# A two-layer convolution block: order of loads and buffers at the seams between passes and in the 7x7 convolution's own steps

## The chip, the core and the metric

The kernel runs on one core of a Trainium2 chip. The core has a matrix engine (TensorE, "PE" in the profile, with its weight loads as "PEld"), a vector engine (VectorE, "DVE"), a scalar engine (ScalarE, "ACT"), GpSimd ("POOL") and SyncE ("SP"), each with its own instruction stream, worked off in the order in which it was written. They wait for one another through semaphores. Transfers between on-chip memory (SBUF) and device memory are started from a stream, here SP's or POOL's (few from ACT's), and are moved by 16 DMA engines. TensorE writes its results to PSUM, in banks of 512 floats per partition, from where another engine evicts them. The metric is the device time of one execution in microseconds (us); lower is better.

## The reference

The input x is 8 images of 96 x 96 points with 192 channels, float32. Two layers are added to it in turn, each of them behind a group norm with 32 groups of six channels.

```python
x = x + layer0(group_norm(x))
x = x + layer1(group_norm(x))

# layer0: 192 -> 384 channels
proj  = v @ W_in + b_in
local = depthwise 3x3 convolution of proj
mixed = 0.25 * (scan right + scan left + scan down + scan up of local) + local
        # scan: s = 0.6 * s + 0.4 * value, along a row or a column
out   = layer_norm(mixed) * ln_g + ln_b, then @ W_out + b_out      # 384 -> 192

# layer1: 192 channels
y = depthwise 7x7 convolution of v, + dw_bias
y = layer_norm(y) * ln_gamma + ln_beta
y = gelu(y @ w0 + b0) @ w1 + b1                                     # 192 -> 768 -> 192
out = y * gamma
```

## The kernel before, in words

The program is a row of passes that hand their data on through device memory[...]. Line numbers are those of the kernel before.

**Pass A** takes the first group norm's figures, normalises and projects to 384 channels, and writes the projection to `P_d`. Per block `k` of rows and per image `b`, `store_a` (L411) issues three whole stores (one per 128 channels, 1152 KB each) and, in the first and the last block, a store of the rows at the blocks' edge (L428), all from POOL.

**Pass B** does the 3x3 convolution as matmuls against banded weight matrices (`conv_b`, L600), 12 channels at a time. `load_b` (L576) reads a banded matrix and, in three pieces, a tile `pin` of `P_d`: the main rows, then one row at each edge, from SP, three blocks ahead. VectorE runs the scans down and up (L633, L642), further matmuls apply the sideways scans as a matrix (L621, L624), and `store_steps` (L644) writes `M_d` from POOL, at the end from SP and POOL.

**Pass C** runs over 192 units u: `load_c` (L984) reads a tile `mt` of `M_d` and a tile `xr` of x, three units ahead, from SP. TensorE transposes and projects (L1008, L1010), ScalarE takes the layer norm's squares (L1014), VectorE forms the new x, in a tile `x1c` of two buffers (L1027), and `store_c` writes it to `X1_d` from SP in pieces of 384 KB (L1063), one per unit. At the head of the pass, inside the pool `c_prep`, weights and norm factors are read and folded into `wc` and `cst` (L949 to L975).

**The own steps.** The 7x7 convolution is again done with banded matrices. The list `todo` has 32 steps: two halves of four images, 16 blocks of 12 channels in each. The first N1 = 19 steps (NI = 16 are one half) stand between pass C and the MLP; the others are mixed into the MLP. A step n has these parts:

- `load_raw(n, t)`, t = 0, 1, 2: rows of x from `X1_d`, half from SP, half from POOL, 384 KB each;
- `scale_steps(n)`: 24 operations that apply the second group norm (tile `xin`, two buffers by parity of n), on VectorE (L841) but for the first and the last of the own steps, where ScalarE does them (L839); and `spread` (L845), which copies the banded matrix to the other 64 partitions on VectorE;
- `load_band(n)` (L820): the banded matrix, 64 partitions x 2496 floats, from SP or POOL by parity. Its tile comes from one of two pools, by parity of n;
- `conv_d(n, c)`, c = 0 to 5: 24 matmuls each (L1168) into two banks, and two evictions on ScalarE (L1178) into `yo`. There are eight banks;
- `store_d(n)`: three stores of `yo` to `Y_d` from SP and three from POOL (L1194, L1198, L1199).

The loop over n that puts these in order begins at L1428. In turn n it stores step n-1, loads the band of n+1 and the rows of n+2, writes the scalings and the spread of n+1, and then the matmuls and evictions of n. In turns 16 and 18 it also writes `load_y` (L1206), which reads the convolved rows back from `Y_d` in 40 small pieces from SP, seven per `conv_d`. In turns 17 and 18, ahead of the matmuls, it writes the first steps of the MLP's layer norm, `norm_steps_e` (L1257): sums, mean, center on VectorE, square on ScalarE, squares on VectorE, powers on POOL, scale on VectorE. The first six or seven of these precede the matmuls of that turn.

Band 0 and the rows of step 0 are read inside pass C, at 20 units before its end, and the rows of step 1 in its last 14 units; the scalings of step 0 are there too.

**The MLP** (L1369, L1379, L1399) runs over tiles of the convolved rows, with the steps 19 to 31 of the convolution in its first half.

In all parts around the change, the order within an engine is the order in which the Python program writes its instructions (`manual_schedule`). Where a pool gives a tile the place of an earlier one, the new tile's first writer waits for the last users of the old one, tile by tile (`reuse_waits="tile"`); where tiles of different pools come to lie on the same bytes, the same holds.

Of the kernel before, what the change touches and what calls it, by code (L numbers as in the profile page):

```python
# [101 lines left out]
def conv_blocks_kernel(  # L102
# [31 lines left out]
    nc = tc.nc  # L134
# [103 lines left out]
    with ExitStack() as ph:  # L238
# [173 lines left out]
        def store_a(po, b, k):  # L412
            at, g = b % GB, b // GB
            for m in range(NC):
                nc.gpsimd.dma_start(
                    P_d[
                        g, m * 128 : (m + 1) * 128, k * WA : (k + 1) * WA, at
                    ].rearrange("p r j h -> p r (j h)"),
                    po[:, m].rearrange("p r j h -> p r (j h)"),
                )  # L420

            for edge, r, row, js in (
                (NK - 1, WA - 1, RB, (0, NJ - 1)),
                (0, 0, RB + 1, (1, NJ)),
            ):
                if k == edge:
                    to = slice(1 - js[0], NJ - js[0])
                    nc.gpsimd.dma_start(  # L428
                        P_d[g, :, row, at, to].rearrange("(m p) j h -> p m (j h)", p=128),
                        po[:, :, r, js[0] : js[1]].rearrange("p m j h -> p m (j h)"),  # L430
                    )

# [128 lines left out]
    by_tile = dict(reuse_waits="tile")  # L561
    with ExitStack() as ph:
# [103 lines left out]
        with tc.manual_schedule():  # L666
# [10 lines left out]
            for n in range(NI * (n_k + 1)):  # L677
                k, i = divmod(n, NI)
                z = None
                if k < n_k:  # L680
# [133 lines left out]
    def load_band(n):  # L814

        i = todo[n][1]
        pool = d_pools[0 if n >= N1 else n % 2]
        bands[n] = band = pool.tile([128, GC, ZW], F32, tag="band", name="band1")
        g = i % 2
        (nc.sync, nc.gpsimd)[g and n < N1].dma_start(  # L820
            band[g * 64 : (g + 1) * 64].rearrange("q c l -> q (c l)"),
            Z2_d[:, i * GC : (i + 1) * GC].rearrange("r c l -> r (c l)"),
        )

    def scale_steps(n):
# [4 lines left out]
        def scale(t, k, b):  # L830
# [7 lines left out]
            if n == 1 or n >= N1 - 1:  # L838
# [17 lines left out]
    gn_pool = ExitStack()  # L856
    gp = gn_pool.enter_context(tc.tile_pool(name="gn", bufs=1, side="right", **by_tile))
# [70 lines left out]
    with ExitStack() as ph:  # L928
# [20 lines left out]
        with tc.tile_pool(name="c_prep", bufs=1, **by_tile) as pp:  # L949
            wo = pp.tile([128, NC, D], F32, name="wo")  # L950
            nc.sync.dma_start(wo, W_out.rearrange("(m p) d -> p m d", p=128))
            gb = pp.tile([128, 2, NC], F32, name="gb")
            with nc.allow_non_contiguous_dma(reason="one value per partition"):
                nc.sync.dma_start(gb[:, 0], ln_g.rearrange("(m p) -> p m", p=128))
                nc.sync.dma_start(gb[:, 1], ln_b.rearrange("(m p) -> p m", p=128))
            bo = pp.tile([128, D], F32, name="bo")
            nc.sync.dma_start(bo, b_out.partition_broadcast(128))
            mean_w = pp.tile([128, 128], F32, name="mean_w")
            nc.vector.memset(mean_w, 1.0 / C)
            lnb = pp.tile([128, NC, 128], F32, name="lnb")  # L960
            ps = ps_s.tile([128, 512], F32, tag="gn_ps", name="ps_w")
            for m in range(NC):
                nc.vector.tensor_scalar(wc[:, m, :D], wo[:, m], gb[:, 0, m : m + 1], None, ALU.mult)
                nc.vector.tensor_copy(lnb[:, m], gb[:, 1, m : m + 1].to_broadcast([128, 128]))
            for m in range(NC):
                nc.tensor.matmul(
                    ps[:, :D], mean_w, wc[:, m, :D], start=(m == 0), stop=(m == NC - 1)
                )
            for m in range(NC):
                nc.tensor.matmul(  # L970
                    ps[:, D : 2 * D], lnb[:, m], wo[:, m], start=(m == 0), stop=(m == NC - 1)
                )
            for m in range(NC):
                nc.vector.tensor_tensor(wc[:, m, :D], wc[:, m, :D], ps[:, :D], ALU.subtract)
            nc.vector.tensor_tensor(cst, bo, ps[:, D : 2 * D], ALU.add)  # L975
# [96 lines left out]
        with tc.manual_schedule():  # L1072
            weights = load_weights()
            for u in range(n_u + 1):
# [7 lines left out]
                if u == n_u - 20:  # L1082
                    load_band(0)
                    for t in range(NT):
                        load_raw(0, t)
# [337 lines left out]
    with tc.manual_schedule():  # L1423
        with tc.tile_pool(name="d_own", bufs=1, side="right", **by_tile) as own:
            d_pools[1] = own
            load_band(1)
            norms, chain = norm_c(1, bank), []
            for n in range(N1):  # L1428
                if n:
                    store_d(n - 1)  # L1430
                    if n + 1 < N1:
                        load_band(n + 1)
# [4 lines left out]
                if n + 1 < N1:  # L1437
                    if n + 2 < N1:
                        for t in range(NT):
                            load_raw(n + 2, t)  # L1440
                    for step in scale_steps(n + 1):
                        step()
                if n >= NI + 1:
                    chain = norm_steps_e(n - NI - 1)
                    for _ in range(7 if n == NI + 1 else 6):
                        chain.pop(0)()
                parts = load_y((n - NI) // 2) if n in (NI, NI + 2) else []
                for c in range(GS):
# [131 lines left out]
```

## Time and profile before

| | |
|---|---|
| time, median of three runs | 5589.31 us (5582.28 to 5594.85) |
| profiled execution | 5586.89 us, its span 5585.1 us |
| PE busy | 5299.5 us (95%), 42206 matmuls |
| DVE, ACT, POOL busy | 3594.6 (64%), 2594.4 (46%), 2326.4 us (42%) |
| DMA | 1015.29 MB, mean 182 GB/s |
| pass A, B, C | to 757, 766 to 1797, 1813 to 2627 us |
| own steps, MLP | 2627 to 3021, 3021 to 5585 us |

The profile is of one execution. Times count from the start of its span. In its lists of waits a line gives the engine, the tile it was about to write and the line of the program, then what ended the wait (engine or DMA and its tile), the total in us, how often, and the longest. In a table of windows the columns are the stretch, its length, the busy time of each engine with the number of instructions, the clock that TensorE was granted as a share of full speed, the mean busy share of the DMA engines and the rate they moved. A share of DMA can come out a little over 1. In the slices, each digit is the busy share of one fortieth of the span in tenths (9 is 90% or more).

### The profile page before, as it was taken

Reading aid. Unit: us, or ns where it says so; the run is one execution under the profiler, and the core shown is the slowest. Engines: PE = TensorE matmul, PEld = TensorE weight load, DVE = VectorE, ACT = ScalarE, POOL = GpSimd, SP = SyncE. Lnnn points to the kernel's source line nnn. Section 1 sums busy time; section 2 is a strip of 40 time slices with the busy share of each in tenths; the row PEclk is TensorE's granted clock in tenths of the full one; section 3 lists DMA queues with packets and bytes.
Section 4 is the critical chain, followed back from the end, with each engine's and each line's share of the span. In section 5 each row is a group of like instructions: output and inputs, shape, how many; then the busy total and the mean of one; then the engine's idle time right before and its main releaser. Section 6 shows DMA issues by size and latency. Waiting matters only on the chain. (4 is left out here: it accounts for less than half of the span.)

```text
span 5585.1 us, 108130 instructions
## 1 busy us (share of the span) xinstructions
PE 5299.5 (95%) x42206; PEld 3348.2 (60%) x42206; DVE 3594.6 (64%) x6714; ACT 2594.4 (46%) x5786; POOL 2326.4 (42%) x2037
## 2 busy tenths in 40 slices
PE   6999989999998999998775999999999999999999
PEld 4666643333333999997342655666566676667667
DVE  6656449999998455555543655555566676766764
ACT  2444447777776566565333444444433233333332
POOL 1111128888887555554321232232233333333332
PEclk9999989999999999999887999999999999999999
DMA  7999869999997899999995554565433332233331
GB/s 217 285 289 268 239 197 245 243 247 243 243 247 207 262 293 288 281 288 270 276 271 130 120 121 110 126 137 140 110 88 92 81 81 77 79 88 90 81 79 40
DMA packets 800700, 1015.29 MB, mean 182 GB/s; under 512 B 331345, under 2 KB 683282, under 8 KB 798141
## 3 DMA queue, kind: packets, MB, share of 16 engines
q1 hardware_dynamic: 712005, 672.30, 47.4%
q0 software_dynamic: 82224, 333.85, 18.4%
q8 instruction: 333, 5.46, 0.4%
q10 hardware_dynamic: 5960, 2.22, 0.2%
q14 instruction: 178, 1.46, 0.1%
HBM read 603.70 MB, written 419.95 MB: 183 GB/s over the span
## 5 line engine op out<-in xcount | busy, mean ns | idle before, releaser
L1399 PEld LDWEIGHTS hp<-w1g,g 128*128 128x128 f32 x6912 | 1118.6, 190 | 141.2 <-issue 73.2
L1399 PE MATMUL hp<-w1g,g 128*128 128x192 f32 x6912 | 1175.6, 329 | 0.0
L1388 ACT ACTIVATE g<-hp,b0g 128x512 f32<-128x512 f32 x864 | 518.3, 690 | 1144.4 <-PE hp L1379 1144.4
L1418 POOL DMA_DIRECT2D out_dram<-xo x288 | 210.5, 731 | 1641.6 <-DVE xo L1410 1546.5
L1369 PE MATMUL hp<-yT,w0w 128*128 128x512 f32 x1728 | 780.8, 598 | 16.0 <-DVE yT L1354 12.1
L1410 DVE TENSOR_TENSOR xo<-hp,r 128x384 f32<-128x384 f32 x288 | 227.6, 790 | 815.2 <-PE hp L1399 806.4
L1010 PE MATMUL po<-wc,mt 128*128 128x193 f32 x3456 | 684.5, 334 | 1.9 <-DVE x1c L1027 1.8
L600 PE MATMUL pl<-pin,band 34*32 34x380 f32 (+1 forms) x13824 | 628.9, 489 | 18.8 <-DMA pin<-P_d 18.8
L674 POOL TENSOR_TENSOR mo<-mo,z 128x768 f32<-128x768 f32 x286 | 598.7, 2093 | 2.7 <-ACT mo L625 0.2
L1168 PE MATMUL hp<-xin,band 63*64 63x372 f32 (+1 forms) x4608 | 441.8, 521 | 154.7 <-DVE band L845 53.4
L1010 PEld LDWEIGHTS po<-wc,mt 128*128 128x128 f32 x3456 | 554.4, 191 | 33.0 <-ACT mean L1012 30.6
L1369 PEld LDWEIGHTS hp<-yT,w0w 128*128 128x128 f32 x1728 | 322.1, 191 | 377.4 <-issue 339.0
L633 DVE TENSOR_TENSOR_SCAN z<-decay,loc 128x768 f32<-128x768 f32 x288 | 505.8, 1756 | 40.8 <-ACT loc L609 11.8
L642 DVE TENSOR_TENSOR_SCAN z<-decay,z 128x768 f32<-128x768 f32 x288 | 498.4, 1731 | 0.1
L600 PEld LDWEIGHTS pl<-pin,band 34*32 34x32 f32 x13824 | 232.8, 107 | 396.8 <-issue 394.8
L1333 POOL TENSOR_TENSOR rs<-tot,neg_half 32x32 f32<-32x32 f32 x72 | 394.6, 5481 | 112.5 <-DVE tot L1331 112.4
L621 PE MATMUL pa<-loc,mix 128*32 128x384 f32 x3456 | 431.8, 493 | 0.0
L624 PE MATMUL pa<-last,down 96*32 96x384 f32 x1152 | 426.7, 493 | 0.9 <-ACT mo L625 0.9
L1168 PEld LDWEIGHTS hp<-xin,band 63*64 63x64 f32 x4608 | 209.7, 145 | 357.5 <-issue 240.4
L1379 PE MATMUL hp<-yT,w0w 64*128 64x512 f32 x1728 | 419.7, 611 | 0.0
L1178 ACT ACTIVATE yo<-hp,dwb 128x384 f32<-128x384 f32 x384 | 200.3, 576 | 437.3 <-PE hp L1168 359.1
L609 ACT COPY loc<-pl 128x384 f32<-128x384 f32 x576 | 248.1, 483 | 311.6 <-PE pl L600 311.6
(158 smaller groups left out, 7524.2 us busy)
## 6 DMA issues: line engine op xcount, KB each, us to landing
P_d<-po POOLq DMA_DIRECT2D x96, 1152.0 KB, 9.7
pin<-P_d SPq DMA_DIRECT2D x192, 576.0 KB
mt<-M SPq DMA_DIRECT2D x192, 384.0 KB
xq<-in_x_dram SPq DMA_DIRECT2D x96, 576.0 KB
xr<-in_x_dram SPq DMA_DIRECT2D x192, 288.0 KB
X<-x1c SPq DMA_DIRECT2D x144, 384.0 KB
r<-X SPq DMA_DIRECT2D x36, 1536.0 KB
out_dram<-xo POOLq DMA_DIRECT2D x288, 192.0 KB, 2.5
```

What stands on the lines that cost most here:

```text
L600: nc.tensor.matmul(pls[g][at * RB : (at + 1) * RB, :, lo:hi], band[rows, c, kh, :], pin[rows, c, :, NJ - 1 - j, lo + kh - 1 : hi + kh - 1] ...
L621: nc.tensor.matmul(pa[at], mix[:, i, at], loc[:, q], start=True, stop=True)
L624: nc.tensor.matmul(pa[at], down[:, to], last[:, q], start=True, stop=True)
L633: nc.vector.tensor_tensor_scan(zf, decay_f, loc.rearrange("p q n -> p (q n)"), 0.0, ALU.mult, ALU.add)
L642: nc.vector.tensor_tensor_scan(zr, decay_f, zr, 0.0, ALU.mult, ALU.add)
L674: eng.tensor_tensor(m, m, z, ALU.add)
L1010: nc.tensor.matmul(po, lhs[m], wc[:, m], start=(m == 0), stop=(m == NC - 1))
L1168: nc.tensor.matmul(pys[g][k * 64 : (k + 1) * 64, :, lo:hi], band[rows, k * GS + c, d * ZS : d * ZS + 64], xin[rows, :, :, k * GS + c, lo + ...
L1369: nc.tensor.matmul(hps[m, q], w0w[:, 0, m * 128 : (m + 1) * 128], yT[:, 2 * q], start=True, stop=False,)
L1379: nc.tensor.matmul(hps[m, q], w0w[p, 1, m * 128 : (m + 1) * 128], yT[p, 1], start=False, stop=True,)
L1388: nc.scalar.activation(g[:, m, q], hps[m, q], AF.Gelu, bias=b0g[:, m : m + 1], scale=1.0)
L1399: nc.tensor.matmul(po[:, q], g[:, m, q, k * 128 : (k + 1) * 128], w1g[:, m], start=(m == 0), stop=(m == NE - 1),)
```

## The change

It has six parts.

1. In the last block of pass A, `store_a` issues the first whole store from POOL, then the edge rows from SP, and then the other two whole stores, one from POOL, one from SP.
2. The weights and norm factors of pass C are read by a new function `load_pre` in pass B, six blocks before its end. Their tiles are views of one tile `c_pre` that has the size of a banded matrix and lies in the pool `gn`, which is opened earlier. The folding into `wc` and `cst` stays at the head of pass C.
3. Band 0 and the rows of step 0 are read one transfer per three units of pass C, beginning 36 units before its end, and band 1 after them.
4. Bands rotate through three pools by n % 3; the third place is the one that `c_pre` had.
5. In the own steps, turn n first issues rows (n+2, 0), then the stores of n-1, then rows (n+2, 1) and (n+2, 2), then the band of n+2.
6. In turn 17 only the first third of step 18's scalings and its spread stand ahead of the matmuls, on VectorE; the other sixteen are on ScalarE, three behind the evictions of each channel. The first three steps of the norm (sums, mean, center) precede the matmuls, and the square, the squares and the powers come behind channels 3, 4 and 5.

```diff
@@ store_a
+            final = b == B - 1 and k == NK - 1
+            whole(0, nc.gpsimd)
+            if not final:
+                for m in range(1, NC):
+                    whole(m, nc.gpsimd)
...
-                    nc.gpsimd.dma_start(
+                    (nc.sync if final else nc.gpsimd).dma_start(
...
+            if final:
+                for m in range(1, NC):
+                    whole(m, (nc.sync, nc.gpsimd)[m % 2])
@@ ahead of pass B
+    gp = gn_pool.enter_context(tc.tile_pool(name="gn", bufs=1, side="right", **by_tile))
+    pre = gp.tile([128, 2 * GS, ZW], F32, tag="band", name="c_pre")
...
+    def load_pre():
+        nc.sync.dma_start(wo, W_out.rearrange("(m p) d -> p m d", p=128))
+        with nc.allow_non_contiguous_dma(reason="one value per partition"):
+            nc.sync.dma_start(gb[:, 0], ln_g.rearrange("(m p) -> p m", p=128))
+            nc.sync.dma_start(gb[:, 1], ln_b.rearrange("(m p) -> p m", p=128))
+        nc.sync.dma_start(bo, b_out.partition_broadcast(128))
@@ loop of pass B
+                if (k, i) == (n_k - 6, 0):
+                    load_pre()
@@ load_band
-        pool = d_pools[0 if n >= N1 else n % 2]
+        pool = early if n >= N1 else (early, gp, d_pools[1])[n % 3]
@@ scale_steps
-            if n == 1 or n >= N1 - 1:
+            if n == 1 or n >= N1 or (n == N1 - 1 and t):
@@ loop of pass C
-                if u == n_u - 20:
-                    load_band(0)
-                    for t in range(NT):
-                        load_raw(0, t)
+                if u == n_u - 36:
+                    early_d = [lambda: load_band(0)]
+                    early_d += [lambda t=t: load_raw(0, t) for t in range(NT)]
+                    early_d += [lambda: load_band(1)]
+                if u >= n_u - 36 and u % 3 == 0 and early_d:
+                    early_d.pop(0)()
+                if u == n_u - 14:
                     first_d += scale_steps(0)
@@ own steps
-            load_band(1)
             for n in range(N1):
+                if n + 2 < N1:
+                    load_raw(n + 2, 0)
                 if n:
                     store_d(n - 1)
-                    if n + 1 < N1:
-                        load_band(n + 1)
+                if n + 2 < N1:
+                    for t in range(1, NT):
+                        load_raw(n + 2, t)
+                    load_band(n + 2)
...
-                if n + 1 < N1:
-                    if n + 2 < N1:
-                        for t in range(NT):
-                            load_raw(n + 2, t)
-                    for step in scale_steps(n + 1):
-                        step()
-                if n >= NI + 1:
-                    chain = norm_steps_e(n - NI - 1)
-                    for _ in range(7 if n == NI + 1 else 6):
-                        chain.pop(0)()
-                parts = load_y((n - NI) // 2) if n in (NI, NI + 2) else []
+                steps = scale_steps(n + 1) if n + 1 < N1 else []
+                now = len(steps) if n + 2 < N1 else len(steps) // NT
+                for step in steps[:now] + steps[-1:] * (now < len(steps)):
+                    step()
+                steps = steps[now:-1]
+                parts = load_y((n - NI) // 2) if n in (NI, NI + 2) else []
+                if n >= NI + 1:
+                    held, chain = chain, norm_steps_e(n - NI - 1)
+                    for step in chain[:3] + held:
+                        step()
+                    chain = chain[3:]
                 for c in range(GS):
                     conv_d(n, c)
                     for step in parts[c * 7 : c * 7 + 7]:
                         step()
+                    for step in steps[c * 3 : c * 3 + 3]:
+                        step()
+                    if n >= NI + 1 and c >= GS - 3:
+                        chain.pop(0)()
```

More of the change, by code (lines that the diff above doesn't have):

```diff
@@ L413, in store_a, with whole @@
             at, g = b % GB, b // GB
-            for m in range(NC):
-                nc.gpsimd.dma_start(
+            final = b == B - 1 and k == NK - 1
+            def whole(m, eng):
+                eng.dma_start(
                     P_d[
@@ L427, in store_a @@
                     to = slice(1 - js[0], NJ - js[0])
-                    nc.gpsimd.dma_start(
+                    (nc.sync if final else nc.gpsimd).dma_start(
                         P_d[g, :, row, at, to].rearrange("(m p) j h -> p m (j h)", p=128),
@@ L561, in conv_blocks_kernel @@
     by_tile = dict(reuse_waits="tile")
+    gn_pool = ExitStack()
+    gp = gn_pool.enter_context(tc.tile_pool(name="gn", bufs=1, side="right", **by_tile))
+    pre = gp.tile([128, 2 * GS, ZW], F32, tag="band", name="c_pre")
+    pre = pre.rearrange("p c l -> p (c l)")
+    wo = pre[:, : NC * D].rearrange("p (m d) -> p m d", m=NC)
+    bo = pre[:, NC * D : (NC + 1) * D]
+    gb = pre[:, (NC + 1) * D : (NC + 1) * D + 2 * NC].rearrange("p (a m) -> p a m", a=2)
+    mean_w, lnb = pre[:, 1024 : 1024 + 128], pre[:, 1152 : 1152 + NC * 128]
+    lnb = lnb.rearrange("p (m k) -> p m k", m=NC)
+    def load_pre():
[4 more added lines that the diff above has]
+        nc.sync.dma_start(bo, b_out.partition_broadcast(128))
     with ExitStack() as ph:
@@ L855, in conv_blocks_kernel @@
     n_s = PH * NV
-    gn_pool = ExitStack()
-    gp = gn_pool.enter_context(tc.tile_pool(name="gn", bufs=1, side="right", **by_tile))
     blk = gp.tile([128, 128], F32, name="blk")
@@ L948, in conv_blocks_kernel @@
             )
[L949 to L975, printed above, removed]
@@ new lines, in conv_blocks_kernel @@
+        nc.vector.memset(mean_w, 1.0 / C)
+        ps = ps_s.tile([128, 512], F32, tag="gn_ps", name="ps_w")
+        for m in range(NC):
+            nc.vector.tensor_scalar(wc[:, m, :D], wo[:, m], gb[:, 0, m : m + 1], None, ALU.mult)
+            nc.vector.tensor_copy(lnb[:, m], gb[:, 1, m : m + 1].to_broadcast([128, 128]))
+        for m in range(NC):
+            nc.tensor.matmul(
+                ps[:, :D], mean_w, wc[:, m, :D], start=(m == 0), stop=(m == NC - 1)
+            )
+        for m in range(NC):
+            nc.tensor.matmul(
+                ps[:, D : 2 * D], lnb[:, m], wo[:, m], start=(m == 0), stop=(m == NC - 1)
+            )
@@ L977, in conv_blocks_kernel @@
+        for m in range(NC):
+            nc.vector.tensor_tensor(wc[:, m, :D], wc[:, m, :D], ps[:, :D], ALU.subtract)
+        nc.vector.tensor_tensor(cst, bo, ps[:, D : 2 * D], ALU.add)
         M_f = [m.rearrange("w c b h -> w c (b h)") for m in M_d]
```

## The prediction

> **What bounds the kernel now.** I read the slices first, to see where TensorE is not full, then the waits, then the windows of those places.
>
> ```profile
> span 5585.1 us, 108130 instructions
> ...
> PE   6999989999998999998775999999999999999999
> ```
>
> Slices are 139.6 us. TensorE is full but for the head (untouched), the seams between passes, and slices 19 to 22 (2513 to 3071), the own steps of the 7x7 convolution. The passes run one after another, so a gain at a seam moves all that follows. Of the waits (total, count, longest) these belong to lines the diff touches, the last one from the window 2550 to 3060:
>
> ```profile
> DVE band L845 <- DMA band<-Z_d: 129.3, 14, 38.9
> PE hp L1168 <- ACT yo L1178: 49.9, 3, 40.8
> PE pl L600 <- DMA pin<-P_d: 18.8, 2, 9.6
> POOL band L820 <- DMA X<-x1c: 18.3, 1, 18.3
> PE ps_w L966 <- DVE wc L963: 15.2, 1, 15.2
> PE hp L1369 <- DVE yT L1354: 12.1, 2, 11.0
> ...
> PE pt L1008 <- DMA mt<-M: 9.2, 1, 9.2
> ```
>
> Then windows: length, busy time of PE, PEld, DVE, ACT, POOL, then clock, DMA share, GB/s.
>
> ```profile
> 757.00:773.00 16.00, 1.45 (x2) 0.17 (x2) 0.00 (x0) 0.30 (x1) 2.68 (x4) 0.60 0.92 323
> 1797.00:1818.00 21.00, 5.77 (x25) 5.09 (x18) 8.34 (x14) 0.76 (x2) 5.46 (x7) 0.60 0.86 247
> 2480.00:2534.00 54.00, 54.00 (x355) 51.03 (x354) 30.29 (x85) 32.62 (x119) 31.27 (x31) 1.00 0.95 294
> 2534.00:2548.00 14.00, 13.77 (x91) 12.82 (x90) 5.66 (x15) 8.04 (x29) 8.07 (x7) 1.00 1.04 234
> 2548.00:2558.00 10.00, 0.84 (x6) 0.57 (x5) 1.44 (x4) 1.10 (x5) 0.86 (x1) 0.71 1.09 238
> 2657.00:2690.00 33.00, 25.98 (x288) 15.04 (x280) 17.82 (x51) 12.61 (x24) 9.18 (x13) 0.91 1.04 301
> 2796.00:2851.00 55.00, 44.67 (x456) 25.30 (x456) 27.60 (x84) 18.91 (x36) 12.86 (x21) 0.84 1.00 279
> 2942.00:2970.00 28.00, 8.94 (x96) 5.50 (x88) 0.00 (x0) 10.43 (x24) 0.00 (x0) 0.68 0.38 95
> 2970.00:3021.00 51.00, 21.27 (x193) 13.01 (x194) 30.55 (x67) 16.15 (x27) 11.40 (x5) 0.65 0.38 91
> 4040.00:5480.00 1440.00, 1440.00 (x6547) 993.38 (x6546) 995.28 (x1866) 457.75 (x637) 496.95 (x267) 1.00 0.32 84
> ```
>
> TensorE waits for DMA at the first seam, at 2548, and through the steps (share 1.0). In the tail (2942 to 3021) DMA is at 0.38, TensorE at 30 of 79 us: a chain of waits. Single times below come from the timeline. After 4040 nothing but TensorE counts, and the change leaves it alone.
>
> **What the Trainium skill says.** "DMA: Bandwidth & Descriptors", section "Issuing engines are not separate DMA queues": a DMA started from another engine shares the same 16 engines and saves only the initiation. The first seam fits: 0.92 busy at 323 GB/s with stores from POOL and loads from SP. The same page, "Anatomy of one DMA": a semaphore is waited for on the issuing sequencer, ahead of everything behind it. The 18.3 us wait of the POOL band load is such a case. The same page, "Where 436 GB/s comes from", has about 358 GB/s for HBM; the steps reach 261 to 301 at share 1.0, so I use the measured rate.
>
> **The change, part by part.**
>
> *Edge rows first.* The last matmul of pass A ends at 756.2; POOL issues three whole stores (0.885 us each), then the edge rows at 758.9, which land near 774; convolution waits for them until 776.5, after two matmuls at 765.8. Now the edge rows, on SP, wait only for evictions done about 751, and go ahead of two whole stores. But in the order of the changed program the last band load still waits for a whole store, and 5.1 MB moved in 757.5 to 772.5. Gain: at most 776.5−765.8 = 10.7, if no wait were left; at least 1, the turn of one POOL store. The bytes before the band rows are the same, and at 323 GB/s they are through near 772, so I take −4.
>
> *Weights of pass C read in pass B.* TensorE idles from 1797.4 to 1812.6; weights are issued 1807 to 1810, but the mt load waits for the last M stores until 1811, and stays. So the removed loads hide behind stores. Three copies (0.165) and three scalings (0.26) go earlier on VectorE, where two scans take 3.49 of each 3.515 us: +1.3. Without that, the gain could be 3. I take −1 (−3 to +1).
>
> *First loads of the steps spread.* Band 0 and three raw loads, 0.64 and 2.36 MB, are issued within 7 us at 2534, and mt is late by 9.2 at 2548 and clock drops (0.8 more). Now they come one per three units (12.4 us), from 36 units before the end, with band 1. Pass C needs 1180 KB per 4.13 us = 286 GB/s, and 309 was reached in 2580 to 2624. A 0.79 MB group costs 2.6 us at 309, of which 12.4×23/309 = 0.9 fits into spare rate: 1.7 late each, some 7 over the five, inside the lead of three units less landing time. I take 8 of 10 gained (3 to 10).
>
> *Band 1 in a buffer of its own.* It is issued at 2647.7 only when the X stores of x1c have landed; the spread ends 2656.4, convolution 1 starts 2656.5. That wait goes. But the third buffer moves the odd xin by 9984 bytes, and it now overlaps the second x1c buffer by 1152. ScalarE's scalings of step 1 (2628 to 2638.6 before) must then wait for those X stores, to 2647.5; behind them on ScalarE are the evictions of convolution 0. 2647.5+10.6 = 2658, the evictions to 2664: convolution 1 starts 7 later. Its POOL and SP stores wait too. Step 3 was due at 2690.7, bound by DMA, and comes at most 2 late. I take +3 (0 to +7).
>
> *Steady steps.* A step starts every 17.4 us, TensorE needs 14. A band takes 13.3 us to land, was issued when the convolution two before ended, and needs 1.45 of spread on VectorE: 129 us of waits. Three buffers give it a further step. The first raw load goes ahead of the Y stores on SP and POOL, the band load behind the other raws; an issue takes SP 0.5 to 2.8 us, under the 14 of TensorE. The scalings still wait for the convolution two before, since xin keeps two buffers. But bytes remain: six raw of 384 KB, a band of 624, Y 2×864, some 4.9 MB; 4.9/17.4 = 281 GB/s, the rate at share 1.0. So the wait for bands becomes one for raw or Y. If a fuller queue gives 2%, 0.35×15 = 5. I take −5 (0 to −15). The DMA engines give a check over these three parts: the rate of 234 instead of 300 for 24 us (5 us), 5% free before 2534 (3), and idle time at 2624 to 2631 that is half usable: 8 to 11; my sum is −10.
>
> *Tail.* Before, counted from the end of convolution 15 (2916.4): Y rows for the first norm land +54, but band 18 is issued behind them on SP (+57), its spread delays sums to +65.3; ScalarE has done all 24 scalings of step 18 ahead of the evictions and stands at the square for 36.0; evictions follow, TensorE stops 40.8; convolution 18 ends +104.4; its stores and the second Y loads let the MLP go on at +132. Now band 18 goes ahead of those loads; eight scalings and the spread are on VectorE ahead of sums, sixteen on ScalarE behind evictions (three of 0.44 and an eviction of 1.05 are 2.4 a channel, TensorE takes 2.3: hidden); sums, mean, center precede the channels, and the square waits until channel 3 is evicted. Sums start at +54; square ends 9.7 later; step 18's xin is ready at +67.6; its convolution ends +81.5. The second Y loads follow the stores of convolution 17, at +67 instead of +83: 15.4 earlier, and they set the MLP's restart. ScalarE still stands at the square, and behind it are the last two evictions and four scalings of step 18, so TensorE stops there still, but for less. Gain 16; 8 if the Y loads pace it, 23 if convolution 18 does. If the first Y rows came 11 later there would be no cover at all.
>
> Sum: −4−1−8+3−5−16 = −31. The profiled run took 5586.9 (span 5585.1 plus 1.8), so 5556; it lies 2.4 under the median of 5589.3, against which I forecast 5558. A measurement can tell about 0.2%, 11 us, from no change.
>
> **Rivals.** (1) *The steps were bound by band latency.* The 14 late bands and 301 GB/s at 2657 speak for it, share 1.0 in each window against. At 301 GB/s a step takes 16.3, at TensorE's bound 14: 15 steps gain 17 to 51, of which 5 are counted: 5512 to 5546; I put it at 5525. (2) *The tail stays paced by its Y loads*: 40 small pieces on SP, which wait for earlier ones (its queue shows 14.0 us on yb<-Y). Fuller DMA queues delay them by the 11 us that remove the gain; then −31+16 = −15, 5574. (3) *Slower: the fuller queue lowers the rate.* Where raw and band were issued together (2534) the rate was 234 at share 1.04. At that rate in the steps, 4.9 MB take 20.9, +3.5×15 = 52, less 26 from the other parts: 5615. It decides below 4.9/(17.4+26/15) = 256 GB/s; against it, 301 at 2657 with the same share. (4) *The change does nothing.* That can be for the weights' read (hidden by stores) and the edge rows (same bytes), hardly for the tail, whose order of work is another; it is inside rival 2.
>
> **How the numbers follow.** Forecast 0.57 (own range 5544 to 5572), rival 1 0.15, rival 2 0.18, rival 3 0.10. Under 5578: the first two but a hundredth, and six tenths of rival 2: 0.82. Over 5600: 0.08. The rest is within 0.2%: 0.10. The range leaves out rival 3 and a few of rival 1's lowest: 5520 to 5585.
>
> **What would show it.** First seam: the pin wait near 5 instead of 9.6, landing near 772. Second: TensorE's gap still about 14. At 2548: mt's wait under 3. Convolution 1 starts later relative to pass C's end, with ScalarE waiting for X stores. Steps: band waits gone, raw or Y waits in their place, period 17. Tail: the 40.8 stop under 27, end of convolution 18 some 23 earlier after convolution 15. It is wrong if the period falls to 15 or rises over 19, if mt waits come back in several pieces, or if Y rows land later than +60.

## The result and the profile after

The changed kernel takes 5572.43 us (median of 20 executions, 5560.3 to 5591.7) where the kernel before takes 5587.11 (20 executions). The ratio is 0.9979, with a 95% interval of 0.997 to 0.9988: 11.7 us faster (6.7 to 16.8; the two medians differ by 14.7). The forecast was 31 us. The sign was right and 5572 lies within the range, but the gain is little more than a third of what was forecast.

In the slices of the profile after, slice 20 (2651 to 2791) has lost a tenth of TensorE time, slices 21 and 22 have gained one each, and slice 29 in the MLP shows 8 in place of 9.

```profile
span 5581.6 us, 108128 instructions
...
PE   6999989999999999998686999999899999999999
```

The list of waits of the changed kernel (total, count, longest) has the lines that answer to those shown of the kernel before. Line numbers are 16 to 29 higher from pass B on.

```profile
PE hp L1187 <- ACT xin L868: 50.2, 8, 27.8
...
PE pl L627 <- DMA pin<-P_d: 20.4, 2, 17.8
ACT xin L868 <- DMA X<-x1c: 18.9, 1, 18.9
POOL raw L839 <- DMA X<-x1c: 18.2, 1, 18.2
...
PE hp L1388 <- DVE yT L1373: 17.6, 3, 11.8
...
DVE band L874 <- DMA band<-Z_d: 16.2, 8, 7.1
...
PE pt L1024 <- DMA mt<-M: 14.9, 5, 10.4
...
PE ps_w L982 <- DVE wc L979: 3.2, 1, 3.2
```

The waits for bands fell from 129.3 to 16.2 us, and the stop of 40.8 us in the tail became one of 27.8, for xin. But the wait for pin is no shorter (20.4 in place of 18.8), the 15.2 at the second seam became 3.2 for the weights and 10.4 for mt, and ScalarE has a new wait of 18.9 for the X stores. The windows (length, busy time of PE, PEld, DVE, ACT, POOL, clock, DMA share, GB/s):

```profile
1797.00:1818.00 21.00, 5.23 (x20) 4.17 (x17) 9.55 (x10) 0.48 (x1) 7.53 (x9) 0.62 0.73 202
2478.00:2540.00 62.00, 53.23 (x322) 49.43 (x321) 29.55 (x80) 29.77 (x108) 30.19 (x30) 0.91 1.06 295
2664.00:2674.00 10.00, 10.00 (x96) 6.53 (x100) 3.28 (x12) 6.20 (x13) 1.98 (x4) 0.75 0.82 183
```

TensorE does 5.23 us of work at the second seam against 5.77 before. Pass C now loses TensorE time in 2478 to 2540, where it lost none before. DMA falls to 183 GB/s early in the own steps.

To compare many profiles I cut each into the same stretches, by instructions in the timeline: the last matmul of pass A; the third matmul of pass B; the last matmul of pass B; the 201st projection of pass C; the first matmul of the own steps; the first Y load on SP; the MLP's first matmul after TensorE's wait of some 11 us for yT (the MLP's restart). The row "conv. 15 to restart" is no stretch of its own: it counts as the prediction counted the tail, from the last eviction of convolution 15, and overlaps the two rows above it. Each column is one execution, in us. Right of the bar are the experiments told below: gentle and burst (early transfers further apart, and in one go), yo_first (result tile first), no_tail (the tail's order undone), two_bands, act_order (evictions ahead), edge (edge rows first, alone), y_twice (more bytes), best_head (first two parts taken back) and best_act (six operations on ScalarE).

```
                       before before  after |gentle burst yo_    no_   two_   act_   edge   y_     best_  best_
                              again                       first  tail  bands  order         twice  head   act
A                       756.2  754.2  754.1 | 754.1  753.9 755.8 756.0  753.7  753.2  755.2  753.4  753.9  754.1
seam A-B                 20.3   20.3   21.8 |  21.9   21.8  21.9  21.8   21.8   21.9   21.9   21.9   20.1   20.1
B                      1020.9 1020.3 1021.2 |1021.6 1021.8 1021.3 1039.8 1021.3 1021.2 1042.6 1021.4 1020.7 1024.2
seam B-C                 66.3   66.5   68.6 |  68.5   72.4  68.8  68.2   68.9   69.0   67.1   68.1   68.7   61.7
C                       763.5  763.0  767.1 | 758.4  760.8 756.5 759.0  757.1  764.4  763.1  759.9  760.1  758.5
steps, to first Y load  304.9  301.7  311.7 | 310.9  301.9 295.7 304.7  299.9  295.8  301.0  352.1  299.1  296.0
tail, to MLP restart    116.5  115.6   95.2 |  95.7   95.9  97.4 102.6  113.3   95.9  114.5   94.6   99.9   98.6
conv. 15 to restart     132.1  131.2  118.4 | 114.8  107.2 107.4 116.7  124.1  106.7  131.1  119.1  112.8  107.0
MLP                    2536.6 2541.1 2542.0 |2542.7 2541.6 2534.6 2538.0 2535.3 2541.5 2537.4 2538.7 2542.6 2544.8
```

Both seams and the steps lost, and the tail gained 20 us. But the mark between steps and tail has moved: the first Y load comes 23.2 us after the last eviction of convolution 15 in the changed kernel, 15.6 before. Counted from that eviction the tail gained 13.7 us. The profiled execution of the changed kernel (5583.44) lies 11 us above its own median, and the table shows one place for it: pass C took 767.1 there and 756.5 to 764.4 in the other profiles whose early loads are the same.

### The profile page after: what moved, and what is told of

Read it like the earlier page. It is cut to its first block, busy times and chain, and to the rows that moved or that the text cites. A ratio compares the mean times of both kernels' runs of the same rounds, so it can differ in the third digit from the quotient of the medians.

```text
span 5581.6 us, 108128 instructions
## 1 busy us (share of the span) xinstructions
PE 5300.3 (95%) x42206; PEld 3355.4 (60%) x42206; DVE 3600.3 (65%) x6722; ACT 2588.8 (46%) x5778; POOL 2320.5 (42%) x2035
## 5 line engine op out<-in xcount | busy, mean ns | idle before, releaser
L1388 PE MATMUL hp<-yT,w0w 128*128 128x512 f32 x1728 | 785.9, 601 | 21.8 <-DVE yT L1373 17.6
L627 PE MATMUL pl<-pin,band 34*32 34x380 f32 (+1 forms) x13824 | 629.0, 490 | 20.4 <-DMA pin<-P_d 20.4
```

What stands on the lines that cost most here:

```text
L627: nc.tensor.matmul(pls[g][at * RB : (at + 1) * RB, :, lo:hi], band[rows, c, kh, :], pin[rows, c, :, NJ - 1 - j, lo + kh - 1 : hi + kh - 1] ...
L1388: nc.tensor.matmul(hps[m, q], w0w[:, 0, m * 128 : (m + 1) * 128], yT[:, 2 * q], start=True, stop=False,)
```

## The experiments

All ratios are to the kernel before, run beside the version in question; 0.1% is 5.6 us.

**Early transfers further apart.**

```diff
-                if u == n_u - 36:
+                if u == n_u - 72:
...
-                if u >= n_u - 36 and u % 3 == 0 and early_d:
+                if u >= n_u - 72 and u % 12 == 0 and early_d:
```

> Changed kernel, with the five early transfers of the own steps started 72 units before the end of pass C and 12 units apart instead of 36 and 3. Theory 1 (pass C leaves DMA too little spare rate: a group of 0.79 MB costs 2.6 us at 309 GB/s, and three units give back 0.9, so five groups use up the lead of mt): 12 units give back 3.5 us, more than a group costs, so TensorE's stalls between 2478 and 2540 (14 us behind by unit 170 in the changed kernel) go, and pass C from its first to its last projection takes about 803 us instead of 815; the whole is 8 to 12 us faster than the changed kernel. Theory 2 (a single blocked queue entry, not the rate, causes the stall, as each raw load waits its turn on SP between mt loads): the stalls stay in size and only come apart, pass C stays at 812 or more, time within 4 us of the changed kernel.

Measured 0.998 (0.997 to 0.9989), the same as the changed kernel, and pass C took 806.2 us from its first to its last projection, 758.4 in the table's stretch. The stalls for mt between 2478 and 2540 are gone and one of 4.1 us stands in their place, for x1c, whose buffers come free when X stores have landed. Theory 1 had the direction; but since the changed kernel's own pass C is as short as 756.5 in another profile, no gain over it is shown.

**Early transfers in one go again.**

```diff
-                if u == n_u - 36:
...
+                if u == n_u - 20:
+                    load_band(0)
+                    for t in range(NT):
+                        load_raw(0, t)
+                    first_d += scale_steps(0)
...
+            load_band(1)
             norms, chain = norm_c(1, bank), []
```

> Changed kernel, with the early transfers of the own steps put back: band 0 and the rows of step 0 in one go at 20 units before the end, band 1 at the head of the own steps. Theory 1 (the bytes cost the same stall however they are put within some 36 units): pass C about 810 us as before the change, 3 to 5 less than the changed kernel, and the first own steps about 2 us later for band 1; the whole within 5 us of the changed kernel. Theory 2 (my prediction's step: the spread takes 8 us off): 8 us slower than the changed kernel.

Measured 0.9988 (0.998 to 0.9996): 5 us slower than the changed kernel by the medians of the ratio, with intervals that overlap. TensorE stops once, 7.9 us for mt, and pass C takes 808.1 from its first to its last projection, as theory 1 had it. The time does not tell the two apart: no gain of 8 us from the spread is shown, and the stretch of pass C is 760.8 here, the average of the versions with the spread. The 72.4 at this profile's second seam, where its first mt came 4 us later than in the others, is not explained.

**The result tile of step 1 first.** This takes away the overlap of xin with x1c.

```diff
+    def new_yo(n):
+        po = d_pools[0 if n >= N1 else n % 2]
+        yos[n] = po.tile([128, NB, NH * NV, GS, WQ], F32, tag="yo", name="yo")
...
-        if c == 0:
-            po = d_pools[0 if n >= N1 else n % 2]
-            yos[n] = po.tile([128, NB, NH * NV, GS, WQ], F32, tag="yo", name="yo")
+        if c == 0 and n not in yos:
+            new_yo(n)
...
+                if n == 0:
+                    new_yo(1)
                 steps = scale_steps(n + 1) if n + 1 < N1 else []
```

> Changed kernel, with the result tile of step 1 allotted ahead of its xin, so that it is the result tile and not xin that overlaps the second x1c buffer by 1152 bytes. Theory 1 (the delay of convolution 1, some 7 us after the overlap, is made up within the steps, which DMA paces): convolution 1 starts about 30 us after the last x1c instead of 34, step 16 at the same distance, time within 4 us of the changed kernel. Theory 2 (it is not made up): 5 to 8 us faster, step 16 that much earlier.

Measured 0.9951 (0.9938 to 0.9964), median 5552.8: the overlap alone cost more than the whole change gained (16 us by the ratios). Convolution 1 starts 18.8 us after pass C in place of 37.4, the steps take 295.7 in place of 311.7. Theory 1, which was the prediction's, falls; theory 2 had the sign and half the size. What the harm is can be read from SP's timeline (start, time of issue, line, transfer), first of the changed kernel:

```profile
2654.62 0.90 SPq L849 DMA_DIRECT2D band<-Z_d  x1
2656.33 0.57 SPq L839 DMA_DIRECT2D raw<-X  x1
2671.75 0.35 SPq L1213 DMA_DIRECT2D Y<-yo  x1
```

and of this one:

```profile
2646.32 0.75 SPq L849 DMA_DIRECT2D band<-Z_d  x1
2647.18 0.57 SPq L839 DMA_DIRECT2D raw<-X  x1
2647.80 0.61 SPq L1216 DMA_DIRECT2D Y<-yo  x1
...
2649.50 12.00 SPq L839 DMA_DIRECT2D raw<-X  x3
```

In the changed kernel SP issues nothing from 2656.9 to 2671.8: the stores of step 0 wait for its evictions, and the next rows and band 3 stand behind these stores, on POOL too. ScalarE shows why the evictions are late:

```profile
2652.70 10.62 ACT L868 ACTIVATE xin<-raw,s 128x192 f32<-128x192 f32 x24 [18.94 <-DMA X<-x1c]
2663.22 3.82 ACT L1197 ACTIVATE yo<-hp,dwb 128x384 f32<-128x384 f32 x8
```

What had been queued kept the DMA engines busy until about 2668, at 243 GB/s; then their share fell to 0.71 and the rate to 145 GB/s until 2676. In 2664 to 2674 it was 183 GB/s; in the other version the same ten microseconds of the steps had 311:

```profile
2655.00:2665.00 10.00, 1.51 (x2) 0.29 (x3) 6.27 (x17) 0.93 (x2) 1.70 (x3) 0.62 1.04 311
```

By 60 us after the first matmul of the own steps DMA has moved 13.3 MB in the changed kernel and 15.9 MB in this version, by 200 us 51.5 and 55.2 MB: the bytes missed are not made up. Why the rate was below 311 already while the engines were busy is not shown.

**Evictions ahead, the overlap kept.** To tell the order on ScalarE from the places of the tiles.

```diff
-                now = len(steps) if n + 2 < N1 else len(steps) // NT
+                now = (len(steps) if n else 0) if n + 2 < N1 else len(steps) // NT
...
-                    for step in steps[c * 3 : c * 3 + 3]:
+                    per_c = 3 if n else 4
+                    for step in steps[c * per_c : (c + 1) * per_c]:
                         step()
```

> Changed kernel, xin of step 1 still overlapping the second x1c buffer, but its 24 scalings on ScalarE are placed four behind each channel's evictions of convolution 0 instead of ahead of them all, so that the evictions no longer stand behind the wait for the X stores. Theory 1 (the harm is the late start: evictions of convolution 0, its Y stores and convolution 1 queued behind the wait): the first evictions come before the X stores have landed, but the later ones still stand behind them; convolution 1 starts 2 to 5 us earlier after pass C than the 37 of the changed kernel, and the time is 2 to 9 us lower. Theory 2 (the places of the tiles themselves, in all odd steps, make the other version faster): no change within 2 us.

Measured 0.9963 (0.9952 to 0.9973), 9 us below the changed kernel by the ratios. Convolution 1 still starts 34.9 us after pass C, yet the stretch of the steps takes 295.8, the same as without the overlap. So theory 1 holds and says more than I had put in it: what counts is when the evictions of convolution 0 let the stores go and the queues move on (SP's gap falls from 15 to 8.4 us, 2654.8 to 2663.2), hardly when convolution 1 starts.

**Two bands again, in the version without the overlap.**

```diff
-        pool = early if n >= N1 else (early, gp, d_pools[1])[n % 3]
+        pool = early if n >= N1 else (early, gp)[n % 2]
...
                     store_d(n - 1)
+                    if n + 1 < N1:
+                        load_band(n + 1)
...
-                    load_band(n + 2)
```

> The version with the result tile of step 1 allotted first, with two band buffers instead of three: band n+1 is loaded in turn n behind the stores of n-1, as before the change, while band 1 is still read in pass C. Theory 1 (the steps move some 83 MB and are bound by the rate; three buffers only keep DMA from running dry, and most of the gain is the earlier start of convolution 1): the stretch from the end of pass C to the first Y load takes 298 to 305 us against 296 with three and 305 before; time 0 to 8 us over the version with three. Theory 2 (a band's latency sets the period, the first rival of the prediction): 308 or more, and 12 us or more over it.

Measured 0.9997 (0.9986 to 1.0007). The steps take 299.9, 4.2 more than with three bands, as theory 1 had it. The time is 26 us over the other by the ratios and 19.5 by the profiles, far more than expected; 15.9 of that is the tail (113.3 in place of 97.4). Its waits, in 2900 to 3060:

```profile
DVE band L874 <- DMA band<-Z_d: 45.3, 2, 36.5
...
PE hp L1190 <- ACT xin L868: 40.8, 1, 40.8
```

The 4.2 are one profile against one, and the four profiles with three bands and without the late evictions lie between 295.7 and 299.1, so they are hardly clear of that spread. Most of what the third buffer is worth here is in band 18, which with it no longer stands behind the Y loads.

**The tail's order undone, band 18 still early.**

```diff
-            if n == 1 or n >= N1 or (n == N1 - 1 and t):
+            if n == 1 or n >= N1 - 1:
...
-                now = len(steps) if n + 2 < N1 else len(steps) // NT
+                now = len(steps)
...
-                    held, chain = chain, norm_steps_e(n - NI - 1)
-                    for step in chain[:3] + held:
-                        step()
-                    chain = chain[3:]
+                    chain = norm_steps_e(n - NI - 1)
+                    for _ in range(7 if n == NI + 1 else 6):
+                        chain.pop(0)()
...
-                    if n >= NI + 1 and c >= GS - 3:
-                        chain.pop(0)()
```

> Changed kernel, with the order of turn 17 put back: all scalings of step 18 on ScalarE ahead of the evictions, the first seven norm steps ahead of the matmuls; band 18 stays ahead of the Y loads. Theory 1 (both halves of the tail change count): TensorE's stop ahead of convolution 18 comes back to about 33 us or more at channel 4 of convolution 17, the second Y loads start some 6 to 9 us later, and the whole is 5 to 9 us slower than the changed kernel. Theory 2 (only band 18's earlier load counts): within 3 us of the changed kernel. Theory 3 (the order carries the whole tail): 12 or more slower.

Measured 0.9993 (0.9982 to 1.0004), 8 us slower than the changed kernel by the ratios, with intervals that overlap. The tail takes 102.6 in place of 95.2, and 94.6 to 99.9 in the eight profiles that keep the order and the early band; TensorE's stop is 31.0 us, under theory 1's 33, and 33.3 in a profile that keeps the order (early transfers in one go). From convolution 15 to the restart it is 116.7, within the 107.2 to 118.4 of the changed kernel and its two variants of the early transfers. So theory 1 has the size of the time, but what the order is worth is not clear of the spread; band 18 is. With the run before this one: the order is worth up to 7 us, band 18 about 16, and the two together 20 to 21.

**More bytes in the steps** (a single execution). SP's main Y store of the first 16 steps goes out twice, once to a tensor that nothing reads.

```diff
+            if k == 0 and n < NI:
+                y_x = dram.tile([NB * m, NH * NV * GS * WQ], F32, name=f"Y_x{n}")
+                eng.dma_start(
+                    y_x.rearrange("(l q) n -> q l n", q=m),
+                    yf[k * 64 + e : k * 64 + e + m],
+                )
```

> Changed kernel, with SP's main Y store (810 KB) of each of the first 16 steps issued twice, the second time to a tensor that nothing reads. Theory 1 (the own steps are bound by what DMA moves, about 280 GB/s): 13 MB more take 46 us, the stretch from the end of pass C to the first Y load goes from 312 to about 350 to 360. Theory 2 (latencies and waits set the period, and DMA has room): under 10 us more.

Measured 352.1 us for the steps, 40 more than the changed kernel (5611.87 in all). In its steps DMA packets of 96.6 MB start, at 274 GB/s and a share of 0.95; in the changed kernel's 83.1 MB at 267 and 0.97, and in those of the kernel before 82.1 MB at 269 and 0.98. The steps are paced by what DMA moves, before the change too.

**Edge rows first, alone on the kernel before.** The edit is part 1 of the change.

> Kernel before, with the first part of the change alone: the edge rows of pass A stored ahead of two whole stores. Theory 1 (the bytes ahead of the third matmul of pass B are the same, and SP, freed earlier, starts the loads of the next blocks beside the last rows of the first): from the last matmul of pass A to the third of pass B about 21.8 us as in the changed kernel against 20.3, time within 3 us of before. Theory 2 (my prediction's step): 16, and 4 us faster.

Measured 1.001 (1.0001 to 1.0019): slower, beyond its interval. The seam takes 21.9 in place of 20.3. Windows of the kernel before, and then of the changed one, at the seam:

```profile
765.00:772.00 7.00, 1.45 (x2) 0.17 (x2) 0.00 (x0) 0.00 (x0) 0.00 (x0) 0.50 1.00 341
772.00:776.00 4.00, 0.00 (x0) 0.00 (x0) 1.25 (x9) 0.00 (x0) 0.00 (x0) 0.50 0.13 45
```

```profile
765.00:772.00 7.00, 0.10 (x1) 0.13 (x2) 1.38 (x10) 0.00 (x0) 0.00 (x0) 0.50 1.03 218
772.00:776.00 4.00, 1.45 (x10) 0.18 (x17) 0.00 (x0) 0.00 (x0) 0.00 (x0) 0.50 0.96 187
```

Before, the stores go through at 341 GB/s and little is left to move while the last rows land. After, SP is free earlier, the band and rows of block 1 (issued at 768.3 on) share the DMA engines with the last rows of block 0, and the rate is 218 and 187. From the last matmul of pass A to the third of pass B 5.47 MB start in place of 5.34, at 251 GB/s in place of 263: the added bytes alone are worth some 0.5 us of the 1.6, by estimate; the rest is the lower rate, whose cause is not shown. The profile of this run shows a second thing: pass B took 1042.6 us. Windows of it and, below, of the kernel before:

```profile
800.00:820.00 20.00, 20.00 (x199) 4.97 (x195) 10.21 (x6) 7.62 (x19) 6.81 (x6) 0.50 0.49 106
```

```profile
800.00:820.00 20.00, 20.00 (x368) 6.98 (x368) 19.37 (x12) 14.51 (x36) 13.52 (x13) 1.00 0.78 167
```

TensorE stayed at half its clock until 841. Of nine profiles with the edge rows first, two show this (this one and that with the tail's order undone), of four without it none. In this run's 22 executions 7 lie at 5599.6 or above; of the 45 of the kernel before beside it none does, the slowest being at 5599.4. This fits 1.6 us and, in some of the executions, 20 more. With the edge rows first TensorE stands in one piece of 17.8 us ahead of pass B, before in two of 9.6 and 9.3 with two matmuls between; that this sets it off is not shown. Other kernels with the edge rows first have such a slow group too (with the early transfers in one go, four of 21 executions take 5587.3 or more, the rest 5578.5 at most), so the changed kernel's times may hold some of this loss, which its own profile does not show.

**First two parts taken back, result tile first.**

```diff
-                if (k, i) == (n_k - 6, 0):
-                    load_pre()
...
+        load_pre()
         nc.vector.memset(mean_w, 1.0 / C)
```

together with `store_a` of the kernel before.

> Changed kernel, with the result tile of step 1 allotted first and the first two parts of the change taken back: edge rows stored last again, weights of pass C read at its head. Theory 1 (edge rows first cost 1.6 us at the seam and, in some executions, 20 us in which pass B starts at half the clock for 75 us instead of 37; the early weights cost 2 us): 3 to 8 us faster than with the result tile alone, thus about 5545 to 5550 where the kernel before takes 5582, and no cluster of times some 20 us above the rest. Theory 2 (these two parts do nothing): within 2 us of it, with the cluster.

Measured 0.9965 (0.9952 to 0.9979), 5564.8. The first seam is 20.1 again. The second part was not taken back in effect: since the tile lies in a pool that is free in pass B, the order that the scheduler made still issues the weights at 1750, and the seam takes 68.7. The run says nothing on the early weights, and the time is no better than with the result tile alone.

**Six operations of the early weights on ScalarE, edge rows last, result tile first.**

```diff
-            nc.vector.tensor_scalar(wc[:, m, :D], wo[:, m], gb[:, 0, m : m + 1], None, ALU.mult)
-            nc.vector.tensor_copy(lnb[:, m], gb[:, 1, m : m + 1].to_broadcast([128, 128]))
+            nc.scalar.activation(wc[:, m, :D], wo[:, m], AF.Identity, scale=gb[:, 0, m : m + 1])
+            nc.scalar.activation(
+                lnb[:, m], gb[:, 1, m : m + 1].to_broadcast([128, 128]), AF.Identity
+            )
```

> As the one with both parts taken back, but with the weights still read in pass B, and the three scalings and three copies of them on ScalarE instead of VectorE. Theory 1 (the early weights lost because their six operations stood on VectorE, which the scans fill, and made the last M stores 2 us late): the seam from pass B's end to the 200th projection of pass C takes 63 to 65 us against 66.3 before and 68.6 after. Theory 2 (the M stores pace the seam in any case): 66 to 67, no gain over the version with the weights at the head.

Measured 0.9958 (0.9945 to 0.997), 5559.1. The row of the seam has 61.7 in place of 68.6, but that overstates the gain: two matmuls of the folding now go ahead of the last matmuls of pass B (at 1794.6), and pass B ends later, with 1024.2 in the table. The two rows together are 1085.9 us, against 1089.8 in the changed kernel, 1089.4 in the run before this one and 1087.2 in the kernel before: a gain of 3.5 to 3.9 over the first two, which is the size that theory 1 asked for, and of 1.3 over the kernel before. VectorE's timeline of the changed kernel at the seam, then POOL's, then VectorE's of the kernel before:

```profile
1792.21 1.97 DVE L979 TENSOR_SCALAR wc<-c_pre 128x192 f32<-128x192 f32 x1
...
1799.07 4.13 DVE L979 TENSOR_SCALAR wc<-c_pre 128x192 f32<-128x192 f32 x2
1803.12 2.29 DVE L701 TENSOR_TENSOR mo<-mo,z 128x768 f32<-128x768 f32 x2
```

```profile
1791.99 2.07 POOL L701 TENSOR_TENSOR mo<-mo,z 128x768 f32<-128x768 f32 x1
...
1800.83 2.01 POOL L701 TENSOR_TENSOR mo<-mo,z 128x768 f32<-128x768 f32 x1
```

```profile
1796.92 5.95 DVE L674 TENSOR_TENSOR mo<-mo,z 128x768 f32<-128x768 f32 x2
...
1812.24 0.78 DVE L963 TENSOR_SCALAR wc<-wo,gb 128x192 f32<-128x192 f32 x3 [9.22 <-DMA gb<-in_L_conv_ln_g_dram]
```

Three scalings that took 0.78 us together, with POOL idle, take 6.1 beside POOL's additions, and they stand ahead of the last additions on VectorE, which release the M stores and with them mt. Not all of the 6.1 is new. In the kernel before, VectorE's own last two additions stood beside POOL's there and took 5.95, where they take 2.29 once POOL is done. So they end 2.5 later than before (1805.4 against 1802.9), and the first mt is issued 2.3 later (1813.7 against 1811.4); that is about the loss of 2.2. The Trainium skill, "SBUF — State Buffer", section "Who interferes with whom", has this: a tensor_scalar can enter a mode of VectorE that takes the port pair it shares with GpSimd, and whichever engine comes second is blocked for the other's whole instruction. The trace agrees: the scalings end at 1794.2 and 1803.2, 0.1 and 0.4 after an addition of POOL ends at 1794.06 and 1802.84.

**The kernel before once more** (a single execution).

> The kernel before once more, unchanged, for the spread of each stage between two profiles: each stage within 3 us of the first profile, the MLP included (2536.6), whose 2542.0 in the changed kernel's profile is not explained.

Every stretch but the MLP is within 3.2 us of the first profile; the MLP took 2541.1, 4.5 more. So the 2542.0 of the changed kernel needs no cause in the change.

## Why the prediction was wrong, point by point

The largest single miss is the overlap of xin with x1c: put at 3 us, it cost some 11. The terms follow in the order of the forecast.

**Edge rows first: −4 forecast, +1.6 measured at the seam.** The step that failed is "the bytes before the band rows are the same, and at 323 GB/s they are through near 772". The bytes are nearly the same (5.47 MB for 5.34), but they were not through by 772: SP, freed earlier, put the loads of block 1 beside them, and the rate fell to 218 and 187 GB/s. I had the order of the loads behind, and looked only ahead of the band rows.

**Early weights: −1 forecast, +2.2 measured** (66.4 to 68.6). That the loads hide behind the M stores was right, and that the six operations go ahead on VectorE too. "Three copies (0.165) and three scalings (0.26)" was the term that was mis-sized: the scalings took 6.1 us beside POOL's additions, not 0.78, and put the last additions 2.5 us back. A duration from a place where POOL was idle was used for one where it is busy. The trace of the kernel before held the sign, two additions of VectorE that took 5.95 us beside POOL.

**Early loads spread: −8 forecast, about −3 measured** (763.2 in three profiles of the old order; 760.3 on average in eight with the spread, 756.5 to 767.1), and even these 3 are not shown to be the spread's: the changed kernel with the transfers in one go took 760.8. The wait of 9.2 for mt went, but not the lost time: in the profile after, it came back in pieces, in the window 1818 to 2640,

```profile
PE po L1026 <- DVE x1c L1043: 6.8, 2, 5.0
...
PE pt L1024 <- DMA mt<-M: 4.5, 4, 1.9
```

with the clock at 0.91 over the 62 us from 2478. "Inside the lead of three units" failed: the X stores share the rate, and x1c, with two buffers, has a lead of its own, which I had not counted. Returning in pieces was one of the signs I had named of being wrong.

**Band 1 and the steady steps: −2 forecast together (+3 and −5), +8 measured in the profile after, +4 on average** (303.3 in two profiles before, and 301.0 in that with the edge rows alone; 311.7, 310.9, 301.9 and 304.7 in the four with the overlap and the first convolution's evictions behind it). The overlap, the wait of ScalarE for the X stores and a convolution 1 that starts 7 later were all foreseen, and the last came out at 8.1 relative to pass C's end. What failed is "step 3 was due at 2690.7, bound by DMA, and comes at most 2 late": convolution 3 starts 70.7 us after the end of pass C in place of 63.6, 7.1 late. In both kernels the steps are bound by DMA, and for that very reason the time of an empty queue is not made up: convolution 4 starts 10.0 later than with the result tile first (96.2 against 86.2), and convolution 16 still 8.5 later (292.9 against 284.4). I wrote that the POOL and SP stores wait too, and did not write what is queued behind them: four of the six raw loads of step 3 and its band. Without that they take 296.7 on average (295.7, 295.8, 299.1 and 296.0, three bands), so it cost some 11 us, where I had put 3. The third buffer itself, 4.2 against 5, agrees with the forecast as far as one profile can tell, and DMA as the bound of the steps is confirmed by the run with more bytes. Against the kernel before, the steady steps make up for the lost time: convolution 16, at 294.0 there, does not start later. Rival 1 is out, since with the bands' waits gone the period is still 17.4 us (convolution 2 to 16; 17.8 and 17.6 in the two profiles before), and rival 3, since the rate over the steps is 267 GB/s, not 234 (269 before).

**Tail: −16 forecast, −13.7 measured as the prediction counts it** (the MLP goes on at +118.4 in place of +132.1), −20.8 from the first Y load (116.0 to 95.2). The steps came as written: convolution 18 ends 82.6 us after the last eviction of convolution 15 (2921.3) against the 81.5 forecast, the stop is 27.8 against "under 27", and the Y loads pace the restart. Sums of their last rows start at +58.8, 5 later than forecast: the first Y load is issued at 2944.5, behind the last raw loads and band 18 on SP (2939.5 to 2943.6), at +23.2 in place of +15.6. This is rival 2 in direction, with 7 us where it had 16; the rest of the gain stays. Of the 20.8, band 18 carries about 16 and the order up to 7.

Added up, by the stretches' averages: +1.6, +2.2, −3, +4, −20.8 and the MLP +3 within its own spread give −13; the measured ratio says −11.7. Of the 18 us between that sum and the forecast, the steps have 6, the first seam 6, pass C 5, the second seam 3 and the MLP 3; the tail gave 5 back. Steps and tail meet at the first Y load, so their 6 and 5 are better read together: 18 forecast, some 17 by these averages, 12.5 in the profile after against the average of the two before. The sign of the result is the tail's alone; the other terms, forecast at −15, add up to no gain.

The version with the result tile first beats both kernels at 0.9951; taking back the edge rows and moving the six operations to ScalarE improves the two seams by 1.8 and, with pass B's later end counted in, 4.2 us in the profile, but the time (0.9958) does not differ from it within the intervals.

## What to carry to other kernels

Where transfers are the bound, as in these steps, a late instruction costs what the transfers queued behind it would have moved in that time; so list what stands behind each store that waits, not only who needs its result. A new buffer moves the tiles allotted after it: look which old tile each of them now overlaps, and choose by the order of allotment which tile has to wait. A duration read where the neighbour engine was idle is no price for the same instruction beside a busy one.

## What the runs showed of the hardware

TensorE's granted clock fell to half in each of the 240 stops of 4 us or more in the thirteen profiles, the one at the start of the program apart, during the stop or within 3 us of its end. The stretches at half clock come in whole multiples of 3.41 us (325 of 338): 10.2 us at 2552 in the kernel before, 34.1 at the first seam in the four profiles with the edge rows last, 37.5 in seven with them first, 75.1 and 81.9 in the other two. After the stop of 9.2 us for mt in the kernel before the clock was full again 4.6 us after the first matmul; after the first seam it took 17 to 20 us from the third matmul of pass B in eleven profiles, and 58 and 64 us in two, with TensorE busy 20.00 of 20 us. The Trainium skill, "TensorE: Matmul & The Clock Gate", section "Part 1: The HAM clock gate", has the full clock come back after about one busy window of 3.4 us; that fits the stop in pass C and not this seam. What differs between the two places, and between 20 and 64 us, these runs don't show.
